# Graph attention on one core: another order of exps, unit ends and gathers, and other engines for the one-hots

## The chip, the cores and the metric

The kernel runs on one core of a Trainium2 chip. A core has a matrix engine (PE, TensorE), a vector engine (DVE), a scalar engine (ACT), GpSimd (POOL) and a sync engine (SP), which works as a queue of DMA starts here. Each engine takes its instructions in order and waits on semaphores of the others. The metric is the device time of one execution in microseconds; the time given is the median of ten.

## What is computed

The reference applies four graph layers in a row to 6250 nodes with 128 features and 100000 edges, sorted by destination. Each stands behind a layer norm and a relu and is added to x:

```python
h = relu(layernorm(x)); x = x + L0(h)   # mean over neighbours, two weights, relu
h = relu(layernorm(x)); x = x + L1(h)   # filter of distances, product over neighbours
h = relu(layernorm(x)); x = x + L2(h)   # three mean layers
h = relu(layernorm(x)); x = x + L3(h)   # three attention layers
```

The change touches the attention, and what is prepared for it during L2. One attention layer, over all edges and one loop per node:

```python
h = x @ W
alpha = leaky_relu((h @ a_src)[s] + (h @ a_dst)[d] + ea_full @ We @ a_edge, 0.2)
ex = exp(alpha - segment_max(alpha, d)[d])
coef = ex / (segment_sum(ex, d)[d] + 1e-16)
out = segment_sum(h[s] * coef[:, None], d) + bias
```

Behind each come a leaky relu and a batch norm over the nodes.

## The kernel before

**Tables.** A node is row p (0 to 124) and column l (0 to 49, `T` = 50) of a table in SBUF. Attention takes its destinations in two parts. The first 3200 nodes (64 rows) are "early": they are summed by matmuls with one-hots. The rest are "late": their edges are gathered one by one.

**Early nodes.** They make five groups (`GP`) of 128 windows. A window holds five nodes (`NW`) and up to 128 edge slots, among them the five loops. For one window PE multiplies two one-hots that have the slots on their 128 partitions. The edge one-hot (128 x 125) says in which row a slot's source lies, weighted by the slot's coefficient; the node one-hot (128 x 250) says to which of five nodes the slot belongs and in which of 50 columns its source lies. The product `cnt` (125 x 250) holds the weights with which table rows go into the window's nodes. `split_edges` (line 2270) walks through 160 steps a layer, 32 a group, each of four windows:

- `ready` (L2420), two steps ahead: it makes node one-hots `hot_n` and edge one-hots `hot_c` and `hot_l`, three buffers of each. Even windows of a step are kept in f32. Odd windows are in the rounded form fp32r and have the coefficient in two parts, `coef_h` and `coef_l`. DVE makes `hot_n` of the even windows by comparing slot numbers with `id_t` (L116); ACT converts those of the odd windows from fp8 tiles that were loaded (L2435), and makes the edge one-hots with the coefficient as scale (L2436); DVE makes `hot_l` of both odd windows at once (L112).
- PE: six `cnt` matmuls of the program (eight rows in the trace, L2623 and L2624). `cnt` has two buffers in PSUM.
- `merged` (L2604): one step later ACT copies `cnt` into `m` (L2607).
- `product` (L2442): eight steps are a unit (32 windows). During the next unit PE multiplies the table by `m` in 50 matmuls (L2447), seven a step. Behind the last, the unit's end: bias on ACT (L2450), leaky relu and batch statistics on DVE (L121, L2452), and a copy into `y_t` on ACT (L2454), all three emitted in step 1 of a unit, ahead of that step's `merged`.
- In the first 20 steps of a group, `source_terms` (L2340) fetches the sources' terms for the next group with small matmuls and reductions on DVE; in the last 12, `softmax` (L2365) makes its coefficients, a piece a step.

**Late nodes.** POOL gathers their edges' table rows with indirect DMAs, 392 a layer, 128 edges each (`fetch`, L2458). `late` (L2477) takes them in blocks of eight: `weights` (DVE: terms, running maximum, exponents), an exp on ACT (L2502), rows times exp on DVE (L112), and eight dependent accumulations on DVE (`acc`, L121), then the store to `late_hist`. It is a generator that advances by 196 pieces in 150 steps, four a block: the exp; rows times exp; four accumulations; four more with the store and `weights` of the block after. Three buffers of rows; `fetch_to` (L2470) releases gathers by the same count, and each is tied to PE's last instruction emitted before it (`clocked`). After the last block comes a serial tail: `late_fix`, then gathers of the sums and the late nodes' ends.

**Ahead of attention.** During L2 a generator `early_edges` (L2030) makes the one-hots in fp8 and stores them in DRAM. `woven` (L1575) interleaves it with PE's units of L2, some nine pieces a unit. Each of 80 iterations handles eight windows: eight `ee_hot` (L2028), one `ee_col` (L2149), four `ee_node` of the odd windows (L2028) and one `ee_hot_t`. A unit of L2 ends with a DVE product `agg` (L112), on which PE's `nt` (L1564) waits a little later.

**What sets the order.** `chain` (L1611) ties the instructions of PE, DVE and ACT in the order in which the program emits them, so an instruction that waits holds up all behind it on its engine. SP's and POOL's follow their queues.

The functions that the diff touches:

Of the kernel before, what the change touches and what calls it, by code (L numbers as in the profile page):

```python
# [22 lines left out]
P = 125  # L23
# [28 lines left out]
def kernel(ctx: ExitStack, tc: tile.TileContext, a: dict, out: bass.AP):  # L52
# [1778 lines left out]
    node_dram = [dram.tile([128, 64 * T * NW], F8, name=f"node{g}") for g in range(GP)]  # L1831
# [10 lines left out]
    class Late:  # L1842
# [3 lines left out]
        def __init__(self, pool):  # L1846
# [12 lines left out]
            self.id_t = pool.tile([128, GP, 128], F32, name="l_id_t")  # L1859
# [170 lines left out]
    def early_edges(lt):  # L2030

        with tc.tile_pool(name="ee", bufs=1) as pool, tc.tile_pool(name="ee_ps", bufs=1, space=PSUM) as ps:
# [59 lines left out]
            for g in range(GP):  # L2092
# [177 lines left out]
    def split_edges(lt, i, first, wp, pool, ps, mv, sc):  # L2270
# [94 lines left out]
        def softmax(g, al_s, of, al, wide):  # L2365

            if not of:
# [41 lines left out]
        def nodes_ready(step):  # L2409

            g, w0 = step // 32, step % 32 * 4
            if w0 % WB == 0:
                lt.hot = pool.tile([128, WB, 128], F8, name="hot")
                nc.sync.dma_start(lt.hot.rearrange("p w h -> p (w h)"), hot_dram[g][:, w0 * 128:(w0 + WB) * 128])
            half_n = pool.tile([128, 2, T * NW], F8, name="half_n")
            nc.sync.dma_start(half_n.rearrange("p w n -> p (w n)"),
                              node_dram[g][:, w0 // 2 * T * NW:(w0 + 4) // 2 * T * NW])
            return half_n

        def ready(step, half_n=None):  # L2420
# [21 lines left out]
        def product(unit, m):  # L2442
# [3 lines left out]
            for l in range(T):  # L2446
                nc.tensor.matmul(o, lhsT=hst[:, l, :D], rhs=m[:P, l, :], start=(l == 0), stop=(l == T - 1))  # L2447
                yield
            z = pool.tile([128, NW, 32], F32, name="z_w")
            nc.scalar.activation(z, o, AF.Identity, bias=bias, scale=1.0)  # L2450
# [3 lines left out]
            nc.scalar.activation(y_t[:, t0:t0 + NW, w0 % P1:w0 % P1 + 32], z, AF.Copy)  # L2454

# [14 lines left out]
        def fetch_to(pieces):  # L2470

            nonlocal fetched
            while fetched < min(C2, 2 * pieces + 16, NB * ((done - 1) // 4 + 3)):
                next(fetches)
                fetched += 1

        def late():  # L2477
# [20 lines left out]
            ahead = weights(0)  # L2498
            for c0 in range(0, C2, NB):
                rows, ex, now = ahead  # L2500
                yield
                nc.scalar.activation(ex, ex, AF.Exp)  # L2502
# [108 lines left out]
        for step in range(steps):  # L2611
# [21 lines left out]
            counted = cnt  # L2633
            if step + 2 < steps:
                hots.append(ready(step + 2))
# [10 lines left out]
            while done < min(4 * (C2 // NB) + 1, (step + 1) * pace):  # L2646
                next(edges_late)
                done += 1
            if done >= 4 * (C2 // NB) + 1:
# [3 lines left out]
        for _ in before:  # L2653
            pass
        before = product(steps // 8 - 1, m)
# [11 lines left out]
        for _ in before:  # L2667
            pass
        held = ps.tile([128, 3, D], F32, name="held", tag="x_ps", bufs=2)
# [475 lines left out]
```

## Time and profile before

| | us |
|---|---|
| median of 10 executions | 4815.62 (4808.55 to 4823.71) |
| the profiled execution | 4825.44 |
| its span, first to last instruction | 4823.0 |
| PE, DVE, ACT, POOL busy | 4160.7, 4043.6, 3306.5, 2851.1 |
| attention layers, about | 2811 to 3471, 3471 to 4135, 4135 to 4795 |

| group of instructions, by form | count | mean ns | idle before it, us, and what ended most of it |
|---|---|---|---|
| L116 DVE `hot_n`, 128x250 | 960 | 363 | 5.3 |
| L112 DVE `hot_l`, 128x250 | 480 | 416 | 1.0 |
| L2435 ACT `hot_n`, 128x250 | 960 | 402 | 27.5, DMA of `half_n` |
| L2436 ACT `hot_c`, 128x125 | 1920 | 391 | 0.1 |
| L2607 ACT `m`, 125x1000 | 480 | 989 | 14.9 |
| L1653 ACT `as_f`, 128x1000 from fp8 | 390 | 1028 | 273.1, DMA of `piece` |
| L2624 PE `cnt` | 2880 | 359 | 122.4, ACT `m` 118.4 |
| L2454 ACT `y_t` | 60 | 339 | 86.6, DVE `z_w` |
| L2502 ACT `ex` | 147 | 213 | 212.4, DVE `ex` 211.8 |
| L2028 DVE `ee_node`, 128x250 | 320 | 363 | 0.4 |
| L67 POOL gathers of `rows`, attention | 1176 | 1015 | 537.2, issue 277.0 |

How to read it: busy time counts an engine as busy while an instruction runs, so neighbours that overlap count once; the mean is that of one instruction, begin to end. On a full engine the next may begin before the last one's recorded end, so start to start can be less than the mean. "Idle before" is the engine's own idle time just ahead of such instructions; what ended it is inferred from semaphores, and "issue" means that the profile shows nothing that was waited for. The view by windows gives per stretch the busy time of each engine with its instructions in brackets, PE's granted clock, the mean busy share of the 16 DMA engines, and GB/s. Lines of the view of waits read: who waits for whom, us in total, times, longest. Lines of the timeline: start, length, engine, line.

### The profile page before, as it was taken

The page shows a single profiled execution, that of the slowest core. Times are in us where ns is not written, and L with a number is a line of the kernel's source. Part 1 is how long each engine was busy: PE and PEld are TensorE (multiplying, and loading weights), DVE is VectorE, ACT ScalarE, POOL GpSimd, SP SyncE. Part 2 cuts the span into 40 slices and gives each one's busy share as a digit, 9 for nine tenths or more (in the row PEclk, how much of TensorE's full clock was granted, in tenths as well). Part 3 has the DMA queues.
Part 4 walks back from the last instruction along what each step waited for, and adds up shares of the span by engine and source line. Part 5 has one row for each costly group of instructions (what it writes and reads, how often), then busy time and mean ns, then how long its engine had stood idle before and what let it go on. Part 6 is the DMA issues. An engine that isn't in the chain of part 4 may idle for free. (4 is left out here: it accounts for less than half of the span.)

```text
span 4823.0 us, 84662 instructions
## 1 busy us (share of the span) xinstructions
PE 4160.7 (86%) x25786; PEld 2987.4 (62%) x25786; DVE 4043.6 (84%) x12029; ACT 3306.5 (69%) x6467; POOL 2851.1 (59%) x2848
## 2 busy tenths in 40 slices
PE   1499998888888869899999979999889999799996
PEld 0255544444444435555555569889779899698896
DVE  7999869999999964677868869899699997798985
ACT  5466658888888857543345567778577778687784
POOL 1365007777777754656737537777367676477772
PEclk9999996666666659999999999999999999899998
DMA  4344336555666647899989955555455554455554
GB/s 99 102 153 157 99 109 221 203 195 204 202 207 201 187 126 223 259 292 277 295 251 295 281 169 162 154 157 155 139 146 156 158 157 136 146 161 153 154 151 111
DMA packets 577362, 868.53 MB, mean 180 GB/s; under 512 B 206555, under 2 KB 451739, under 8 KB 568450
## 3 DMA queue, kind: packets, MB, share of 16 engines
q1 hardware_dynamic: 483459, 674.15, 44.0%
q0 software_dynamic: 91104, 186.95, 15.0%
q8 instruction: 205, 3.36, 0.3%
q10 hardware_dynamic: 2332, 1.93, 0.2%
q14 instruction: 262, 2.15, 0.1%
HBM read 563.92 MB, written 298.68 MB: 179 GB/s over the span
## 5 line engine op out<-in xcount | busy, mean ns | idle before, releaser
L67 POOL DMA_INDIRECT rows<-gtable,l_src x1176 | 1193.1, 1015 | 537.2 <-issue 277.0
L67 POOL DMA_INDIRECT rows<-table,f_src x784 | 781.2, 996 | 282.4 <-issue 231.5
L2447 PE MATMUL o<-m,hst 125*128 125x160 f32 x6000 | 916.7, 304 | 0.0
L67 POOL DMA_INDIRECT s_rows<-table,s_src x660 | 659.5, 999 | 346.4 <-issue 164.2
L2624 PE MATMUL cnt<-hot_n,hot_c 128*125 128x250 f32 x2880 | 755.3, 359 | 122.4 <-ACT m L2607 118.4
L2447 PEld LDWEIGHTS o<-m,hst 125*128 125x128 f32 x6000 | 855.4, 194 | 0.0
L1653 ACT ACTIVATE as_f<-piece 128x1000 fp32r<-128x1000 fp8e4 x390 | 380.7, 1028 | 273.1 <-DMA piece<-adj 183.9
L2624 PEld LDWEIGHTS cnt<-hot_n,hot_c 128*125 128x125 f32 x2880 | 450.2, 192 | 160.4 <-ACT m L2607 130.4
L2607 ACT ACTIVATE m<-cnt 125x1000 f32<-125x1000 f32 x480 | 474.7, 989 | 14.9 <-PE cnt L2624 13.4
L923 PE MATMUL z<-w,s 128*128 128x128 f32 x1568 | 347.3, 391 | 153.2 <-DVE s L121 148.6
L2623 PE MATMUL cnt<-hot_n,hot_l 128*125 128x250 f32 x960 | 453.3, 472 | 0.0
L121 DVE SCALAR_TENSOR_TENSOR acc<-acc,ex,rows 128x130 f32<-128x130 f32 x1173 | 414.5, 353 | 33.8
L923 PEld LDWEIGHTS z<-w,s 128*128 128x128 f32 x1568 | 294.5, 281 | 232.9 <-DVE s L121 232.3
L1544 PE MATMUL o<-as_f,of_two 128*128 128x500 f32 x1560 | 415.1, 412 | 13.1 <-ACT as_f L1653 11.9
L1407 ACT ACTIVATE adj<-cnt 128x1000 fp8e4<-128x1000 f32 x250 | 305.5, 1222 | 176.0 <-PE cnt L1406 170.3
L2435 ACT ACTIVATE hot_n<-half_n 128x250 fp32r<-128x250 fp8e4 x960 | 386.4, 402 | 27.5 <-DMA half_n<-node 27.1
L2436 ACT ACTIVATE hot_c<-hot,coef_t 128x125 f32<-128x125 fp8e4 x960 | 375.6, 391 | 0.1
L2436 ACT ACTIVATE hot_c<-hot,coef_h 128x125 fp32r<-128x125 fp8e4 x960 | 374.9, 391 | 0.0
L902 PE MATMUL z<-bf,w 128*128 128x512 f32 x392 | 354.3, 1002 | 8.9 <-ACT bf L868 8.9
L1544 PE MATMUL o<-adj,parts 128*128 128x500 fp8e4 x1500 | 358.6, 377 | 0.1
L1544 PEld LDWEIGHTS o<-as_f,of_two 128*128 128x128 f32 x1560 | 295.4, 192 | 85.0 <-ACT as_f L1653 16.5
L868 ACT ACTIVATE soft<-z 128x512 f32<-128x512 f32 x392 | 222.0, 586 | 164.2 <-PE z L923 163.7
(628 smaller groups left out, 8114.2 us busy)
## 6 DMA issues: line engine op xcount, KB each, us to landing
piece<-adj SPq DMA_DIRECT2D x360, 250.0 KB
late_hist<-acc SPq DMA_DIRECT2D x147, 455.0 KB
dist<-ew_dram SPq DMA_DIRECT2D x48, 1024.0 KB
sum_hist<-s_acc SPq DMA_DIRECT2D x132, 320.0 KB
adj<-adj SPq DMA_DIRECT2D x10, 3125.0 KB
hot<-hot SPq DMA_DIRECT2D x240, 128.0 KB
half_n<-node SPq DMA_DIRECT2D x480, 62.5 KB
ea<-in_edge_attr SPq DMA_DIRECT2D x54, 512.0 KB
```

What stands on the lines that cost most here:

```text
L67: return nc.gpsimd.indirect_dma_start(out=dst, out_offset=None, in_=table, in_offset=bass.IndirectOffsetOnAxis(ap=idx, axis=0))
L121: nc.vector.scalar_tensor_tensor(o, x, s, y, op0=op0, op1=op1)
L902: nc.tensor.matmul(z1, lhsT=w1, rhs=st["bf"][:, i % 2 * HB:(i % 2 + 1) * HB, :], start=False, stop=True)
L923: nc.tensor.matmul(z2[:, j, :], lhsT=s1[:, j, :], rhs=w2, start=False, stop=j == HB - 1)
L1544: yield nc.tensor.matmul(o[:, :n], lhsT=parts.columns(l, 1, s)[:, 0, :], rhs=adj(l), start=(l == 0 and s == 0), stop=(l == T - 1 and s == ...
L1653: nc.scalar.activation(made[-1], piece[:, at:at + n], AF.Copy)
L2435: nc.scalar.activation(hot_n[k][:, h, :], half_n[:, h, :], AF.Copy)
L2436: nc.scalar.activation(hot_c[k][:, h, :], hot[:, w, :], AF.Copy, scale=(high if k else coef)[:, w0 + w:w0 + w + 1])
L2447: nc.tensor.matmul(o, lhsT=hst[:, l, :D], rhs=m[:P, l, :], start=(l == 0), stop=(l == T - 1))
L2607: nc.scalar.activation(m[:P, :, :, u * 4:u * 4 + 4].rearrange("p l k q -> p k l q"), cnt[:P, :, :T * NW].rearrange("p w (k l) -> p k l w", ...
L2623: nc.tensor.matmul(o, lhsT=hot_l[:, h, :], rhs=hot_n[k][:, h, :], start=True, stop=False)
L2624: nc.tensor.matmul(o, lhsT=hot_c[k][:, h, :], rhs=hot_n[k][:, h, :], start=k == 0, stop=True)
```

## The change

- Node one-hots are now made ahead for all windows. In `early_edges` DVE compares four windows at once (128x1000, both operands spread), twice in each of the 80 iterations, in place of four comparisons; the table in DRAM and its stores double. `id_t` (f32, kept) becomes `id_b` (bf16, in the pool of that stage).
- In `ready`, ACT converts the node one-hots of two windows at a time (500 columns), even and odd ones alike; the tile `half_n` holds four windows. DVE weights the edge one-hots in pairs, by a product with the spread coefficients.
- A unit's end becomes a generator in three parts, run in steps 1, 2 and 4 of a unit, behind `merged`.
- `late`: `weights` of the next block stands before the accumulations, its exp among them, so that the pieces of a block are: rows times exp; `weights`; four accumulations; exp and four more with the store. The last piece of a block is one later than before. The store is one DMA in place of two.
- `fetch_to`: up to 20 gathers ahead in place of 16, with the rule of buffers shifted by one piece; that rule now binds.
- `softmax`: one more pause among its five exps, from the second group on.

```diff
@@ early_edges
-                for x, x_t in ((hi, hi_t), (lo, lo_t), (place, lt.id_t[:, g, :])):
+                id_b = pool.tile([128, 128], BF16, name="ee_id_b")
+                for x, x_t in ((hi, hi_t), (lo, lo_t), (place, id_b)):
...
-                    node = pool.tile([128, WB // 2, T * NW], F8, name="ee_node", bufs=2)
-                    for w in range(0, WB, 2):
-                        n = w0 + w + 1
-                        one_hot(node[:, w // 2, :], slot_b, lt.id_t[:, g, n:n + 1])
-                    nc.sync.dma_start(node_dram[g][:, w0 // 2 * T * NW:(w0 + WB) // 2 * T * NW],
-                                      node.rearrange("p w n -> p (w n)"))
+                    for n0 in range(w0, w0 + WB, 4):
+                        node = pool.tile([128, 4, T * NW], F8, name="ee_node", bufs=2)
+                        nc.vector.tensor_tensor(node, slot_b[:, None, :].to_broadcast([128, 4, T * NW]),
+                                                id_b[:, n0:n0 + 4, None].to_broadcast([128, 4, T * NW]), OP.is_equal, saturate=False)
+                        nc.sync.dma_start(node_dram[g][:, n0 * T * NW:(n0 + 4) * T * NW], node.rearrange("p w n -> p (w n)"))
@@ softmax
                                      accum_out=node[:, 1, k:k + 1])
+                if parted and k == NW // 2:
+                    yield
@@ nodes_ready
-            half_n = pool.tile([128, 2, T * NW], F8, name="half_n")
+            half_n = pool.tile([128, 4, T * NW], F8, name="half_n")
@@ ready
-            for w in range(4):
-                k, h = w % 2, w // 2
-                if k == 0:
-                    ts(hot_n[k][:, h, :], lt.slot[:, :T * NW], lt.id_t[:, g, w0 + w:w0 + w + 1], OP.is_equal)
-                else:
-                    nc.scalar.activation(hot_n[k][:, h, :], half_n[:, h, :], AF.Copy)
-                nc.scalar.activation(hot_c[k][:, h, :], hot[:, w, :], AF.Copy,
-                                     scale=(high if k else coef)[:, w0 + w:w0 + w + 1])
+            by = hot.rearrange("p (h k) c -> p k h c", k=2)
+            for k, of in enumerate((coef, high)):
+                nc.scalar.activation(hot_n[k], half_n.rearrange("p (h k) n -> p k h n", k=2)[:, k], AF.Copy)
+                tt(hot_c[k], by[:, k], of[:, w0:w0 + 4].rearrange("p (h k) -> p k h", k=2)[:, k, :, None].to_broadcast([128, 2, P]), OP.mult)
@@ product, its end
+            ends.append(unit_end(unit, g, w0, o))
+        def unit_end(unit, g, w0, o):
             z = pool.tile([128, NW, 32], F32, name="z_w")
             nc.scalar.activation(z, o, AF.Identity, bias=bias, scale=1.0)
+            yield
             stt(z, z, 0.01, z, OP.mult, OP.max)
             nc.vector.bn_stats(stats[:, unit, :], z.rearrange("f k q -> f (k q)"))
+            yield
             t0 = w0 // P1 * GP * NW + g * NW
             nc.scalar.activation(y_t[:, t0:t0 + NW, w0 % P1:w0 % P1 + 32], z, AF.Copy)
@@ fetch_to
-            while fetched < min(C2, 2 * pieces + 16, NB * ((done - 1) // 4 + 3)):
+            while fetched < min(C2, 2 * pieces + 20, NB * ((done - 2) // 4 + 3)):
@@ late
             ahead = weights(0)
+            yield
+            nc.scalar.activation(ahead[1], ahead[1], AF.Exp)
+            yield
             for c0 in range(0, C2, NB):
                 rows, ex, now = ahead
+                more = c0 + NB < C2
+                tt(rows, rows, ex[:, 0, :, None].to_broadcast([PL, NB, W]), OP.mult)
                 yield
-                nc.scalar.activation(ex, ex, AF.Exp)
+                if more:
+                    ahead = weights(c0 + NB)
                 yield
                 acc = pool.tile([PL, NB, W], F32, name="acc")
-                tt(rows, rows, ex[:, 0, :, None].to_broadcast([PL, NB, W]), OP.mult)
-                yield
                 for j in range(NB):
+                    if j == NB // 2:
+                        yield
+                        if more:
+                            nc.scalar.activation(ahead[1], ahead[1], AF.Exp)
...
-                    if j == NB // 2 - 1:
-                        yield
                 nc.vector.tensor_copy(acc[:, :, AL], now)
-                bulk(bass.AP(tensor=late_hist.tensor, offset=late_hist.offset + c0 * W, ap=[[C2 * W, PL], [1, NB * W]]),
-                     acc.rearrange("p c f -> p (c f)"))
-                if c0 + NB < C2:
-                    ahead = weights(c0 + NB)
-            yield
+                nc.sync.dma_start(bass.AP(tensor=late_hist.tensor, offset=late_hist.offset + c0 * W, ap=[[C2 * W, PL], [1, NB * W]]),
+                                  acc.rearrange("p c f -> p (c f)"))
+                yield
@@ the steps
                 merged(step - 1, m, counted)
             counted = cnt
+            if u in (1, 2, 4):
+                end_some()
```

`end_some` runs one part of the oldest unit's end; behind the loop all that are left are run.

More of the change, by code (lines that the diff above doesn't have):

```diff
@@ L1830 @@
     of_dram = [dram.tile([128, NW * WCAP], BF16, name=f"of{g}") for g in range(GP)]
-    node_dram = [dram.tile([128, 64 * T * NW], F8, name=f"node{g}") for g in range(GP)]
+    node_dram = [dram.tile([128, 128 * T * NW], F8, name=f"node{g}") for g in range(GP)]
     ale_dram = [[dram.tile([128, WCAP], F32, name=f"ale{i}_{g}") for g in range(GP)] for i in range(3)]
@@ L1858, in __init__ @@
             self.slot = pool.tile([128, C2], F32, name="l_slot")
-            self.id_t = pool.tile([128, GP, 128], F32, name="l_id_t")
             self.vecs = [pool.tile([128, 6], F32, name=f"l_vecs{i}") for i in range(3)]
@@ L2365, in softmax @@
         def softmax(g, al_s, of, al, wide):
+            parted = not of
             if not of:
@@ L2414, in nodes_ready @@
                 nc.sync.dma_start(lt.hot.rearrange("p w h -> p (w h)"), hot_dram[g][:, w0 * 128:(w0 + WB) * 128])
-            half_n = pool.tile([128, 2, T * NW], F8, name="half_n")
-            nc.sync.dma_start(half_n.rearrange("p w n -> p (w n)"),
-                              node_dram[g][:, w0 // 2 * T * NW:(w0 + 4) // 2 * T * NW])
+            half_n = pool.tile([128, 4, T * NW], F8, name="half_n")
+            nc.sync.dma_start(half_n.rearrange("p w n -> p (w n)"), node_dram[g][:, w0 * T * NW:(w0 + 4) * T * NW])
             return half_n
@@ L2448, in product, with end_some @@
                 yield
+            ends.append(unit_end(unit, g, w0, o))
+        ends = []
+        def unit_end(unit, g, w0, o):
             z = pool.tile([128, NW, 32], F32, name="z_w")
             nc.scalar.activation(z, o, AF.Identity, bias=bias, scale=1.0)
+            yield
             stt(z, z, 0.01, z, OP.mult, OP.max)
             nc.vector.bn_stats(stats[:, unit, :], z.rearrange("f k q -> f (k q)"))
+            yield
             t0 = w0 // P1 * GP * NW + g * NW
             nc.scalar.activation(y_t[:, t0:t0 + NW, w0 % P1:w0 % P1 + 32], z, AF.Copy)
+        def end_some():
+            if ends:
+                if next(ends[0], 0) == 0:
+                    ends.pop(0)
         NB, given, order = 8, [], Pace(0)
@@ L2645, in split_edges @@
             fetch_to((step + 1) * pace)
-            while done < min(4 * (C2 // NB) + 1, (step + 1) * pace):
+            while done < min(4 * (C2 // NB) + 2, (step + 1) * pace):
                 next(edges_late)
                 done += 1
-            if done >= 4 * (C2 // NB) + 1:
+            if done >= 4 * (C2 // NB) + 2:
                 for _ in islice(edges_late, 2):
@@ L2654, in split_edges @@
             pass
+        while ends:
+            end_some()
         before = product(steps // 8 - 1, m)
@@ L2668, in split_edges @@
             pass
+        while ends:
+            end_some()
         held = ps.tile([128, 3, D], F32, name="held", tag="x_ps", bufs=2)
```

## The prediction

> **What bounds the kernel now.** I read the page first (span 4823.0 us; PE 86%, DVE 84%, ACT 69% busy), then busy time by windows, because the two stages that the change touches have different limits. First the loop of the first attention layer, one window for each of its five groups of 32 steps:
>
> ```profile
> core 0: us, PE busy (x) PEld busy (x) DVE busy (x) ACT busy (x) POOL busy (x), PEclk, DMA share, GB/s
> 2856.00:2975.00 119.00, 101.73 (x939) 95.42 (x940) 109.64 (x330) 95.37 (x266) 89.45 (x88) 0.94 0.57 157
> 2975.00:3095.00 120.00, 111.65 (x1045) 105.77 (x1044) 105.85 (x319) 89.99 (x249) 85.51 (x85) 0.99 0.56 155
> 3095.00:3214.00 119.00, 110.68 (x1042) 105.34 (x1041) 107.39 (x325) 93.39 (x260) 87.26 (x83) 0.97 0.56 156
> 3214.00:3330.00 116.00, 110.33 (x1044) 105.53 (x1043) 107.76 (x324) 91.51 (x253) 85.01 (x84) 0.99 0.59 161
> 3330.00:3434.00 104.00, 98.18 (x647) 93.97 (x646) 74.44 (x243) 86.29 (x233) 59.96 (x61) 0.97 0.46 127
> ```
>
> PE and DVE are equally full in four groups of five; only in the last, which prepares no next group, DVE is light. The two other layers look alike. Next who waited for whom in the first four groups, 2856 to 3330 us:
>
> ```profile
> ACT ex L2502 <- DVE ex L121: 65.7, 32, 4.2
> ...
> PE cnt L2624 <- ACT m L2607: 36.3, 18, 5.1
> ACT y_t L2454 <- DVE z_w L121: 23.7, 14, 4.0
> ...
> DVE coef_l L112 <- ACT coef_t L2405: 6.2, 4, 2.4
> DVE z_w L121 <- ACT z_w L2450: 5.6, 5, 3.1
> DVE al L112 <- issue: 5.4, 24, 0.6
> ```
>
> So PE stalls on `merged` (ACT m), because ACT, which works in order, stands before it at an exp or a unit's end that waits for DVE. The engine waited for in the end is DVE. DVE itself hardly waits: 430.6 us busy of 474, and of the 43.4 idle this view names 22.8; the rest are gaps between dependent instructions too short to be listed.
>
> Second, the layers before (1860 to 2811 us), where the one-hots are made beside PE's matmuls; three windows, each from one `agg` of a unit to the next:
>
> ```profile
> 2480.50:2508.80 28.30, 28.30 (x130) 17.97 (x129) 12.12 (x45) 16.47 (x19) 5.23 (x4) 1.00 0.79 222
> ...
> 2543.30:2573.40 30.10, 29.73 (x133) 18.22 (x132) 28.39 (x97) 16.86 (x19) 23.08 (x24) 1.00 0.99 313
> ...
> 2668.80:2700.90 32.10, 30.21 (x130) 18.78 (x129) 30.08 (x103) 17.16 (x21) 21.78 (x22) 0.95 0.98 292
> ```
>
> PE sets the pace, but in the busy units DVE is 94% full and the DMA engines 98%, while in others DVE is half empty.
>
> **Part 1, the edge and node one-hots in the loop.** A step loses two DVE instructions (node one-hots, L116) and four on ACT (edge one-hots, L2436), and gains two products on DVE; the two ACT copies of 250 become two of 500. The new products have the form of today's `hot_l` (128x250, fp8 times a spread f32). What counts on a full engine is start to start:
>
> ```profile
> 2999.26 1.23 DVE L112 TENSOR_TENSOR rows<-rows,ex 128x1040 f32<-128x1040 f32 x1
> ...
> 3000.41 0.60 DVE L116 TENSOR_SCALAR hot_n<-l_slot,l_id_t 128x250 f32<-128x250 f32 x2
> ...
> 3000.93 0.41 DVE L112 TENSOR_TENSOR hot_l<-hot,coef_l 128x250 fp32r<-128x250 fp8e4 x1
> ...
> 3001.26 0.57 DVE L112 TENSOR_TENSOR one<-x_ps,col 128x400 f32<-128x400 f32 x1
> ```
>
> Two one-hots take 3000.93-3000.41 = 0.52 us, one product 3001.26-3000.93 = 0.33. Two products less two one-hots: +0.14 us a step, 4.5 a group, 17.9 over four groups. ACT is relieved: 2x402+4x391 = 2368 ns a step before; a copy of 500 lies between the rows of 250 (402) and 1000 (1028 ns, L1653), about 610, so 1220 after. ACT is not the limit, so this saves only what its lateness costs. The node tiles read double: at a DMA share of 0.57 I cost it at nothing; ACT waited for them 27.1 us in all, and with ACT early that wait has cover. If not, 28 waits of 1 us are the price.
>
> The Trainium skill, "VectorE: DVE Perf Modes", perf-mode tier table, lets `tensor_scalar` run at twice the rate of `tensor_tensor` in fp32, which speaks against this swap. This trace does not agree: 250 elements in 0.26 us is one a cycle of its 0.96 GHz. By the page a one-hot would take about (58+125)/0.96 = 0.19 us (estimate) and the swap would cost 0.14 us a step more, 18 us a layer; I go by the rows.
>
> **Part 2, the order of exp, `weights` and unit ends.** The order of the built kernel puts `weights` a step ahead of its exp, and a unit's end on ACT, DVE, ACT in three different steps. ACT's 65.7 and 23.7 us of waiting go; so do DVE's waits for ACT: 6.2 + 5.6 + 0.9 (`rows` for ex) = 12.7 us. What is late next is DVE. Four groups: 430.6 + 17.9 busy, 43.4 - 12.7 = 30.7 idle that stays, 479.2 against 474: **+5.2 us a layer**. Bounds: -13 (the swap hidden) to +18 (no wait goes).
>
> **Part 3, gathers and last group.** `fetch_to` now releases the eight gathers of a block together, when the block three before is done, and `weights` wants them a piece earlier: six pieces, 4.6 steps, some 17 us, after release. They take 8x(0.95+0.30) = 10 us on POOL, 2.3 to 3.0 to land (chain of waits), and wait for PE's last matmul of their step, up to 3.7. That is 13 to 17 of 17, so DVE will wait now and then: I take **+3 a layer** (0 to +40, a wait of 1 us at each of 40 blocks). In the last group gathers bind already (8.1 us of waits of `al` there). The last block's `weights` now stands ahead of the previous block's eight accumulations, which came first before: 8 x 0.38 (row of `acc`: 414.5+33.8 us by 1173) = **+3 a layer** into the serial tail (0 to +3). PE's stall on `merged` in the last group, 4.8 us in the first layer, goes, but only some lies on the path: **-2** (-5 to 0). The late table's store as one DMA saves an issue of SP, off the path; the extra pause in softmax ends two steps before its coefficients are wanted: nothing.
>
> Sum in attention: 3 x (5.2+3+3-2) = **+28 us**.
>
> **Part 4, node one-hots for all, in the layers before.** 80 times, four one-hots of 250 become two operations of 1000:
>
> ```profile
> 2363.74 0.56 DVE L2149 TENSOR_TENSOR ee_col<-ee_slot_b,ee_lo_t 128x400 fp8e4<-128x400 bf16 x1
> 2364.23 1.91 DVE L121 SCALAR_TENSOR_TENSOR s_acc<-s_acc,s_same,s_rows 128x128 f32<-128x128 f32 x5
> 2366.06 1.20 DVE L2028 TENSOR_SCALAR ee_node<-ee_slot_b,l_id_t 128x250 fp8e4<-128x250 bf16 x4
> 2367.18 0.96 DVE L2028 TENSOR_SCALAR ee_hot_t<-ee_rows,ee_here 128x1024 fp8e4<-128x1024 uint8 x1
> ```
>
> `ee_col` has the new form: 400 elements in 0.49 us. `rows` above does 1040 in 1.15, so an element costs 0.66/640 = 1.04 ns and 1000 cost 1.11. Two: 2.22 against 1.12 to 1.16 for the four: +1.08 us, x80 = **86 us of DVE** from 2060 to 2760. I added it to each of the 22 windows between `agg`s (0 to 5 iterations in each). The sum exceeds the window in ten, by 18 us together (30.10: 28.39+5.40 = 33.8; 32.10: 35.5); if DVE can fill only 95%, as in its fullest window, by 36 in twelve. PE then waits at `nt<-agg`, where it already waits 20.9 us in the run. The other windows swallow the rest. The doubled stores add 80 x 128 KB = 10.2 MB; in windows at a share of 0.96 to 1.00 and some 310 GB/s each iteration's 0.128 MB costs 0.4 us, some 16 us in nine windows, mostly the same ones that DVE lengthens, so not added. I take **+30** (0 to 86).
>
> **Sum.** 28 + 30 = +58. The profiled execution took 4825.4 us (span 4823.0), 0.2% over the median 4815.6 of the ten runs; it would take 4883, and the median **4874 us**. Own range with the bounds of the parts mixed: 4830 to 4915.
>
> **Rivals.** (a) *The order wins.* PE's idle time for `merged` is 118.4 us in the page. If DVE's idle time is mostly slack and not gaps, ACT's freedom returns half of it and the lulls before hide part 4: 4815.6 - 59 = **4757**. It decides once DVE's work with its gaps stays under PE's 111 us a group; against it stands the fourth group, 116 us with DVE busy 107.8 before 4.5 are added. (b) *Hidden on both sides*: -4 and 0, **4812**. Against it: the 94% windows. (c) *Part 4 at full price*, since waits of DVE for ACT and SP's in-order queue (`piece` loads stand behind the node stores, which wait for DVE) spoil the lulls: 28 + 86, **4930**. (d) *Late gathers* at every block of four groups, 1 us each: 4874 + 3 x 37 = **4985**; for it, the 13 to 17 of 17 us; against it, a stalled DVE falls back towards PE, which shortens the wait for PE.
>
> **Chances.** Forecast 0.48, (a) 0.13, (b) 0.13, (c) 0.19, (d) 0.07. About 0.2%, 10 us, can be told from no change: faster 0.13, same 0.13, slower 0.74. The range leaves out (d) and most of (a): 4800 to 4935.
>
> **What would show it.** Right: DVE at 94% or more in the first four groups, 114, 110, 112 and 112 us busy; ACT under 60% there with no waits of `y_t` for `z_w`; groups of 117 to 121 us; `ee_node` 2.2 us a pair, units at 2543 and 2668 longer by 3 to 5 us with PE waiting for `agg`. Wrong: groups of 112 us with PE at 98% (a); units unchanged (b); `al` waiting for `rows` over 10 us a layer (d). A product of fp8 by f32 faster than 0.33 us would also undo it.

## The result and the profile after

The changed kernel takes **4942.97 us** (median of 8 runs, 4936.09 to 4955.84) against 4817.29 for the kernel before in the same comparison (28 runs): ratio **1.0265**, 95% interval 1.0255 to 1.0275. It is slower, as forecast, by twice the forecast: 126 us for 58. The profiled execution has a span of 4945.1 us (before 4823.0, +122.1).

Three marks in the trace divide these 122 us (1.2 us more lie outside the rows): the first `ee_node`, the first `hot_l` of a layer, and the first matmul into `held` behind its loop and tail.

| stretch | before | after | difference |
|---|---|---|---|
| start to first `ee_node` | 2059.7 | 2054.9 | -4.8 |
| first `ee_node` to first `hot_l` (the layers before) | 797.0 | 858.1 | **+61.1** |
| first `hot_l` to `held`, three layers | 614.6, 611.1, 612.1 | 631.6, 632.6, 638.2 | **+64.6** |

So both halves are larger than forecast: 61 for 30, and 65 for 28. A stretch is read from one profiled execution. How far to trust it shows in runs on such chips that leave a stretch's code as it was: the layers before took 797.0, 790.9 and 793.5 us, attention 1837.8, 1841.4 and 1837.7, and the start, which no edit touches, 2038 to 2060.

**The layers before.** The view by windows over the second stretch, first of the kernel before, then of the changed one (columns: window, length, then busy time and instructions of PE, PEld, DVE, ACT and POOL, PE's granted clock, DMA share, GB/s):

```profile
2059.70:2856.70 797.00, 759.50 (x3802) 463.24 (x3801) 604.36 (x2017) 379.46 (x507) 424.83 (x428) 0.98 0.87 271
```

```profile
2054.90:2913.00 858.10, 777.56 (x3801) 471.79 (x3799) 688.18 (x1856) 379.85 (x506) 489.61 (x427) 0.95 0.86 264
```

PE does the same 3801 matmuls. Its idle time grows from 37.5 to 80.5 us (+43.0), and the matmuls themselves take 18.1 us longer, at a mean clock of 0.95 in place of 0.98: 43.0 + 18.1 = 61.1, all of it. The waits name who is late, first in the kernel before (2055 to 2765 us), then in the changed one (2055 to 2820 us):

```profile
PEld nt L1564 <- DVE agg L112: 16.0, 11, 4.4
...
PE nt L1564 <- DVE agg L112: 8.3, 5, 3.6
```

```profile
PEld nt L1564 <- DVE agg L112: 62.8, 16, 6.9
...
PE nt L1564 <- DVE agg L112: 50.1, 15, 6.1
```

PE's matmuls wait for the end of a unit on DVE 15 times in place of 5, for 41.8 us more: nearly all of the 43.0. Why a wait also makes the matmuls slower shows in three short windows around one of these pauses (5.4 us, ended at 2409.8 by `agg`); columns: window, length, PE busy with its matmuls in brackets, clock, DMA share, GB/s.

```profile
2404.00:2410.00 6.00, 0.58 (x2) 0.71 0.86 253
2410.00:2414.00 4.00, 4.00 (x10) 0.58 0.80 239
2414.00:2418.00 4.00, 4.00 (x22) 1.00 0.94 306
```

For some 4 us behind the pause PE is granted 0.58 of its clock and gets through ten matmuls, and then through 22 in as long. By the trace's clock record, which holds only the full and the half clock here, the half clock is granted for 37.5 us in 7 stretches of this part before, and for 88.7 us in 17 after. PE is busy for 29.9 and 68.4 us of that; half of the 38.5 us more is 19.2, about the 18.1 by which the matmuls got longer.

**Attention.** The five groups of the first layer in the changed kernel:

```profile
2913.00:3031.00 118.00, 101.57 (x940) 94.30 (x940) 105.22 (x311) 68.79 (x126) 85.89 (x84) 0.96 0.59 170
3031.00:3151.00 120.00, 110.66 (x1032) 103.98 (x1031) 109.83 (x326) 69.70 (x127) 83.25 (x84) 0.97 0.58 169
3151.00:3270.00 119.00, 110.13 (x1026) 103.90 (x1026) 108.19 (x318) 70.71 (x127) 86.21 (x82) 0.97 0.59 172
3270.00:3391.00 121.00, 111.72 (x1037) 105.16 (x1036) 109.13 (x326) 69.71 (x127) 85.49 (x84) 0.97 0.58 170
3391.00:3500.00 109.00, 100.17 (x649) 92.75 (x648) 76.35 (x246) 65.52 (x112) 63.48 (x62) 0.98 0.49 145
```

ACT is at 58%, as meant. But DVE is not full: 432.4 us busy of 478 in the first four groups (90%), and even in the last group, where DVE is 70% busy, the loop got longer. The waits of the first four groups (longer ones of ACT and POOL left out at the top):

```profile
...
ACT hot_n L2433 <- DMA half_n<-node: 67.8, 37, 5.7
POOL rows L67 <- PE x_ps L2356: 33.3, 17, 6.0
...
ACT ex L2525 <- DVE ex L121: 25.1, 13, 6.1
DVE al L112 <- DMA rows<-gtable,l_src: 24.5, 17, 3.8
PE x_ps L2356 <- DMA hot_t<-hot_t: 20.3, 12, 5.8
```

and in the kernel before, in its first four groups (2857 to 3326 us):

```profile
POOL rows L67 <- PE x_ps L2357: 10.6, 13, 1.6
...
DVE al L112 <- DMA rows<-gtable,l_src: 2.3, 12, 0.2
...
PE x_ps L2357 <- DMA hot_t<-hot_t: 2.0, 4, 0.8
```

ACT's waits for DVE went for the most part, as forecast (`ex` 65.7 to 25.1, `y_t` is gone), and PE's wait for `m` with them (36.3 to 6.2). In their place DVE waits for gathered rows, 24.5 us here and 17.0 in the last group, against 2.3 and 8.1 before; and PE waits for loads of `hot_t`. These share SP's queue with loads of `hot`, which wait for a buffer that DVE still reads (SP waits 91.6 us for `hot_l` there); that this is what delays them is not shown.

Some of the runs below were on chips on which the kernel before itself takes 5344 to 5413 us, with waits of PE named issue that the runs shown so far don't have. They are kept apart, under 4, and no difference in time is taken across.

### The profile page after: what moved, and what is told of

Read it like the earlier page. It is cut to its first block, busy times and chain, and to the rows that moved or that the text cites. A ratio compares the mean times of both kernels' runs of the same rounds, so it can differ in the third digit from the quotient of the medians.

```text
span 4945.1 us, 81847 instructions
## 1 busy us (share of the span) xinstructions
PE 4204.7 (85%) x25786; PEld 3000.2 (61%) x25786; DVE 4156.0 (84%) x11869; ACT 2978.4 (60%) x4547; POOL 2933.8 (59%) x2848
## 5 line engine op out<-in xcount | busy, mean ns | idle before, releaser
L67 POOL DMA_INDIRECT rows<-gtable,l_src x1176 | 1209.0, 1028 | 575.9 <-issue 307.4
L67 POOL DMA_INDIRECT s_rows<-table,s_src x660 | 719.7, 1090 | 335.1 <-issue 163.9
L2433 ACT ACTIVATE hot_n<-half_n 128x500 f32<-128x500 fp8e4 x960 | 539.2, 612 | 301.3 <-DMA half_n<-node 300.3
L118 DVE TENSOR_SCALAR run<-acc,f_same,f_fresh 128x128 f32<-128x128 f32 (+1 forms) x783 | 313.2, 400 | 14.4
L1544 PE MATMUL o<-piece,of_three 128*128 128x500 fp8e4 x1200 | 290.0, 385 | 2.2 <-ACT of_three L1121 1.7
```

Source lines behind the costliest of these rows:

```text
L67: return nc.gpsimd.indirect_dma_start(out=dst, out_offset=None, in_=table, in_offset=bass.IndirectOffsetOnAxis(ap=idx, axis=0))
L118: nc.vector.tensor_scalar(o, x, s1, s2, op0=op0, op1=op1)
L1544: yield nc.tensor.matmul(o[:, :n], lhsT=parts.columns(l, 1, s)[:, 0, :], rhs=adj(l), start=(l == 0 and s == 0), stop=(l == T - 1 and s == ...
L2433: nc.scalar.activation(hot_n[k], half_n.rearrange("p (h k) n -> p k h n", k=2)[:, k], AF.Copy)
```

## The experiments

The question is which part costs what. The theory after the traces: part 4 costs the layers before 61 us through DVE, and attention is set by late gathers. Rivals: DVE's extra products are the whole loss in attention; the doubled stores are that of part 4.

**1. The one-hots alone (parts 1 and 4), and the order alone (parts 2 and 3).** The changed kernel is cut in two: `early_edges`, `nodes_ready` and `ready` are those of after in the one, and of before in the other; all else goes the other way.

> The one-hot parts alone (1 and 4) once more, since in the first call the kernel before took 5411 us, 12% more than in its shown runs, with waits of TensorE named issue that those runs do not have. Expected where the kernel before takes 4816 us: theory (part 4 costs the layers before 55 us, the new order most of the rest): first hot_n load 55 us later, attention +10 to +25 us in all, about 4890 us. Rival (VectorE's extra products are the loss in attention): attention +55 to +70, about 4935 us.

> The new order alone (parts 2 and 3), once more for the same reason. Theory (late gathers are the price in attention): the layers before as before, waits of al for rows 25 to 45 us a layer, attention +20 to +40 us, about 4845 us. Rival (VectorE's extra products): attention 0 to -20, about 4805 us. Rival (a) of the prediction: 4757 us.

| | time (ratio, its interval) | before there | first `ee_node` to `hot_l` | three layers | DVE waits ahead of `al`, by layer |
|---|---|---|---|---|---|
| one-hots alone | 4914.11 (1.0213, 1.0194 to 1.0233) | 4815.02 | 862.7 (+65.7) | 1861.6 (+23.8) | 19.7, 18.0, 20.9 |
| order alone | 4823.52 (1.0022, 1.0011 to 1.0033) | 4815.02 | 790.9 (-6.1) | 1857.2 (+19.4) | 42.5, 46.2, 41.9 |
| both: the change | 4942.97 | 4817.29 | 858.1 (+61.1) | 1902.4 (+64.6) | 41.6, 44.6, 44.5 |
| (before) | | | 797.0 | 1837.8 | 16.9, 15.3, 12.7 |

Part 4 alone accounts for the layers before. In attention each half costs some 20 us, and both together 21 more than their sum. DVE's waits for rows come with the order: some 131 us in three layers with it, 45 before, and 59 with the one-hots alone. The rival (products are all) falls: it wanted 55 to 70 in the first row and a gain in the second. The one-hots alone took 4914 in place of the 4890 expected: part 4 took 66 and not 55, and the median lies 8 us above the profiled run. The order alone took 4824 in place of 4845: its waits for rows came as the theory said, and cost the least that it had allowed.

**2. Rows in time.** A fourth buffer for gathered rows, and the release a block earlier, in the changed kernel and in the order alone (which, so that it fits, also has one buffer in place of two for the products on the way to `al_s`):

```diff
-                    given.append(pool.tile([128, NB, W], F32, name="rows", bufs=3))
+                    given.append(pool.tile([128, NB, W], F32, name="rows", bufs=4))
-            while fetched < min(C2, 2 * pieces + 20, NB * ((done - 2) // 4 + 3)):
+            while fetched < min(C2, 2 * pieces + 28, NB * ((done - 2) // 4 + 4)):
```

> The changed kernel with four buffers of gathered rows in place of three, and gathers released a block earlier (ten pieces ahead of the weights, not six). Theory (late gathers cost attention what the order alone lost, 19 us, and the 21 us that order and one-hots lost together beyond their sum): waits of al for rows fall from 42 to 20 us a layer or less, attention 40 us shorter than in the changed kernel, about 4903 us. Rival (VectorE is full, and fills the time it no longer waits with its delayed work; or the loads behind it in SP's queue set the pace): within 10 us of 4943 us.

> The new order with the old one-hots, with four buffers of gathered rows and the earlier release (and one buffer in place of two for the products on the way to al_s, so that it fits). Theory (late gathers are what the order lost): waits of al 15 us a layer as before the change, attention 20 us shorter than with the order alone, and shorter than before the change by what ScalarE's freedom is worth, 0 to 30 us in all: about 4800 us. Rival (the gathers' waits only fill time in which VectorE would wait for others): 4815 to 4830 us.

The changed kernel with rows in time takes **4851.26** (before 4815.43; ratio 1.0080, interval 1.0063 to 1.0097), 92 us less than without, more than twice what was expected. Attention takes 599.0, 600.2 and 601.4 us a layer: 101.8 less than the change, and 37.2 less than before it. The first four groups:

```profile
2910.00:3365.00 455.00, 425.95 (x4047) 402.43 (x4046) 430.79 (x1276) 277.79 (x503) 349.57 (x338) 0.99 0.62 180
```

```profile
ACT hot_n L2433 <- DMA half_n<-node: 60.7, 36, 6.2
...
PE x_ps L2356 <- DMA hot_t<-hot_t: 6.3, 10, 1.2
...
DVE al L112 <- DMA rows<-gtable,l_src: 3.1, 3, 2.3
```

Now DVE is 95% busy (430.8 of 455): here is the full DVE that the prediction had taken for granted. PE's waits for `hot_t` shrank from 20.3 to 6.3 without any edit to those loads, so most of them followed from the late rows. (SP's waits for `hot_l` fell less, from 91.6 to 75.9.) ACT's waits for `half_n` are nearly as long as in the changed kernel and seem to cost nothing: ACT has 177 of 455 us to spare. And PE's clock is back at 0.99.

The order alone with rows in time takes **4733.22** (ratio **0.9840**, interval 0.9819 to 0.9861), 82 us faster than the kernel before: a version that beats both. Attention takes 1754.4 us, 83.4 less than before. Its first four groups:

```profile
2832.00:3275.00 443.00, 423.35 (x4044) 401.20 (x4042) 417.70 (x1277) 364.60 (x1011) 339.00 (x338) 0.99 0.59 166
```

PE is 96% busy, so little is left there to win. The three terms of attention can be read off now: order with rows in time -83.4, one-hots on top +46.2 (1800.6 - 1754.4), late rows on top +101.8; their sum is +64.6. The first includes whatever the buffer would be worth without the order.

The two pairs also show what a wait of DVE for rows costs here. In the changed kernel its waits ahead of `al` fell from 130.7 to 33.0 us in the three layers, by 97.7, and attention by 101.8. In the order alone they fell from 130.6 to 26.4, by 104.2, and attention by 102.7. So the price was the length of the waits, nearly one for one.

**3. What part 4 pays with.** The kernel before with one half of part 4's cost each: four more one-hots an iteration to a spare tile, or every node store issued twice.

```diff
+                    spare = pool.tile([128, WB // 2, T * NW], F8, name="ee_spare", bufs=2)
+                    for w in range(0, WB, 2):
+                        one_hot(spare[:, w // 2, :], slot_b, lt.id_t[:, g, w0 + w:w0 + w + 1])
```

```diff
+                    nc.sync.dma_start(spare_dram[g][:, w0 // 2 * T * NW:(w0 + WB) // 2 * T * NW],
+                                      node.rearrange("p w n -> p (w n)"))
```

> The kernel before with four more one-hots of 250 in each of the 80 iterations of the layers before, written to a spare tile that nothing reads: VectorE's added time of part 4 (1.12 us an iteration against 1.08), without its doubled stores. Theory (VectorE's time is the price of part 4): first hot_n load 45 to 60 us later, attention unchanged, about 4868 us. Rival (the doubled stores, which keep the next node tile and the loads behind them waiting, are half of it or more): 25 us or less, about 4835 us.

> The kernel before with each store of node one-hots issued a second time, to a table that nothing reads: the doubled stores of part 4 without VectorE's added time. Theory (VectorE's time is the price of part 4): 0 to 10 us, about 4820 us. Rival (the stores): 25 to 50 us, about 4850 us.

DVE's time alone: 4879.43 (ratio 1.0130, interval 1.0112 to 1.0148); the stretch takes 858.7, +61.7. That is the whole of part 4's price. The stores alone: 4856.58 (1.0091, interval 1.0074 to 1.0109); the stretch takes 836.0, +39.0, where 0 to 10 were expected. So each alone costs much, and both together no more than DVE's alone. A likely reason is that a PE that waits for DVE gives the transfers the time that they need: in the changed kernel ACT waits less for its adjacency pieces than before, 99.9 us for 167.5. It was not tested by itself. With the stores alone these waits are the ones that grow most. Of PE's idle time there, 27.3 us more than before, 10.9 are waits for what ACT makes of the pieces, 5.5 for pieces themselves and 9.4 for `agg` (ACT's waits of the kernel before from 2055 to 2765 us, then with doubled stores from 2044 to 2800 us):

```profile
ACT as_f L1653 <- DMA piece<-adj: 167.5, 54, 12.5
```

```profile
ACT as_f L1653 <- DMA piece<-adj: 264.6, 77, 12.2
```

**4. Runs on the other chips** (before at 5344 to 5413 us). They cover the two halves of the change and the changed kernel with rows in time (the same kernels as above), the unit's end alone, the buffer alone, the buffer with the unit's end, the old order with gathers released as in the change, and the faster version with another release. The edits that are new:

```diff
@@ old order, gathers of a block released together, six pieces ahead
-            while fetched < min(C2, 2 * pieces + 16, NB * ((done - 1) // 4 + 3)):
+            while fetched < min(C2, 2 * pieces + 24, NB * ((done - 3) // 4 + 3)):
@@ old order, four buffers
+            while fetched < min(C2, 2 * pieces + 24, NB * ((done - 1) // 4 + 4)):
@@ new order, four buffers, two gathers a piece
+            while fetched < min(C2, 2 * pieces + 22, NB * ((done - 2) // 4 + 4)):
```

The two halves of the change, and the changed kernel with rows in time:

> The one-hot parts alone (parts 1 and 4: all node one-hots made and stored in the layers before, converted on ScalarE; edge one-hots weighted in pairs on VectorE), with the old order of exp, weights, unit ends and gathers. Theory (two separate prices: the layers before lose 55 us to part 4; in attention the changed kernel loses most of its 65 us to the gathers, which the new order releases later): first hot_n load 55 us later than before, attention only +10 to +25 us in all three layers, VectorE waiting for rows no more than before (15 us a layer), about 4890 us. Rival (VectorE's extra products are the whole loss in attention): attention +55 to +70 here too, about 4935 us.

> The new order alone (parts 2 and 3: unit ends in three steps, softmax pause, weights a step ahead of its exp, gathers released in whole blocks), with the one-hots made as before. Theory (late gathers are the price in attention): the layers before as before; VectorE waits for rows 25 to 45 us a layer as in the changed kernel, attention +20 to +40 us, about 4845 us. Rival (VectorE's extra products): attention 0 to -20, about 4805 us. Rival (a) of the prediction, the order wins half of PE's waits: about 4757 us.

> The changed kernel with four buffers of gathered rows in place of three, and gathers released a block earlier to match. Theory (late gathers are the price in attention): waits of al for rows fall from 42 us a layer to 17 or less, attention gains 30 to 50 us in all, about 4905 us. Rival (VectorE's extra products, or the loads behind them in SP's queue): rows arrive in time but PE waits as long, within 10 us of 4943 us.

The unit's end alone:

> Only the unit's end in three steps and the pause in the softmax; late edges, gathers and one-hots as before. Theory (ScalarE's waits for z_w, 24 us in the first four groups of a layer, hold up the merge of the counts, on which PE waits 36 us there): PE's waits on m fall by a third, 5 to 10 us a layer gained, about 4795 us. Rival (VectorE sets the end, PE's waits are slack): within 0.2% of before, 4806 to 4825 us.

The buffer alone, and with the unit's end:

> The kernel before with the fourth buffer of gathered rows and the earlier release alone (nine pieces ahead of the weights), old order, old one-hots. Theory (the old order had its rows 5 to 13 us early, so the buffer is worth little without the new order; the gain of the order with the buffer, 82 us, is the order's): waits of al fall by 5 us a layer, 0 to 15 us gained, about 4808 us. Rival (the buffer is the gain, in any order): attention 60 to 85 us shorter, about 4740 us.

> The kernel before with the fourth buffer of gathered rows and the earlier release alone, once more, since in the call before this one the kernel before took 5402 us. Theory (the old order had its rows 5 to 13 us early, so the gain of the order with the buffer is the order's): 0 to 15 us gained, about 4808 us. Rival (the buffer is the gain, in any order): attention 60 to 85 us shorter, about 4740 us.

> The kernel before with the fourth buffer of gathered rows and the earlier release alone. Where the kernel before takes 4816 us: theory (the old order had its rows 5 to 13 us early, so the gain of the order with the buffer is the order's): 0 to 15 us gained, about 4808 us. Rival (the buffer is the gain, in any order): attention 60 to 85 us shorter, about 4740 us. Where it takes 5410 us: again 30 us slower, as in the two runs there.

> The same with the unit's end in three steps and the pause in the softmax, late edges in the old order. Theory (of PE's 36 us of waits on m in the first four groups of a layer, the exps that wait for weights on VectorE cause more than the unit ends do, by their waits of 66 to 24 us): a quarter of the order's gain, 15 to 30 us, about 4790 us. Rival (the unit ends on ScalarE are the larger part): 50 us or more, 4765 us or less.

> The same with the unit's end in three steps and the pause in the softmax, late edges in the old order, once more for the same reason. Theory: a quarter of the order's gain, 15 to 30 us, about 4790 us. Rival (the unit ends on ScalarE are the larger part): 50 us or more, 4765 us or less.

The release in eights in the old order:

> The kernel before, old order and old one-hots, with its gathers released as in the change: the eight of a block together, six pieces ahead of its weights. Theory (the late release costs by itself): waits of al of 30 us a layer or more, attention 20 to 60 us longer, about 4850 us. Rival (the release costs only together with the new order, in which ScalarE no longer waits for VectorE): within 10 us of before, about 4816 us.

> The kernel before, old order and old one-hots, with its gathers released as in the change: the eight of a block together, six pieces ahead of its weights. Where the kernel before takes 4816 us: theory (the late release costs by itself): waits of al of 30 us a layer or more, attention 20 to 60 us longer, about 4850 us. Rival (it costs only together with the new order): within 10 us of before, about 4816 us. Where it takes 5410 us: again 5% slower, as in the run there.

The faster version, two gathers a piece:

> The new order with the old one-hots and four buffers of gathered rows, its gathers released two a piece, the last of a block seven pieces ahead of the weights, and no longer eight at once. Where the kernel before takes 4816 us: theory (what counts is that rows arrive in time): as fast as with whole blocks, 4725 to 4745 us; rival (the early first gathers are needed): 4760 us or more. Where it takes 5410 us: theory (there the burst of eight gathers is what costs 5%): 5350 to 5440 us; rival (it is the order): 5650 us or more.

| kernel, and how it releases gathers | ratio to before there |
|---|---|
| one-hots alone, two a piece | 1.0023 |
| unit's end alone, two a piece | 0.9994 |
| buffer alone, two a piece, three runs | 1.0061, 1.0067, 1.0078 |
| buffer and unit's end, two a piece, two runs | 1.0065, 1.0098 |
| new order with buffer, two a piece | 0.9986 |
| old order, eight at once, six pieces ahead, two runs | 1.0509, 1.0535 |
| new order alone, eight at once | 1.0520 |
| changed kernel with rows in time, eight at once | 1.0564 |

None of these ratios can stand for the chips of the result: there the one-hots alone cost 1.0213 (here 1.0023) and the order alone 1.0022 (here 1.0520). What was forecast for these chips came about: the buffer alone 29 us slower for 30, the release in eights 5.1% for 5, and two a piece 5342 us, just under the 5350 to 5440 of the theory and far from the 5650 of its rival. The unit's end brought nothing that can be told from none here, alone (0.9994) or beside the buffer (1.0065 and 1.0098). The rows part into two classes, by one property: whether eight gathers are released at once. The new order with four buffers is at 0.9986 with two a piece, and in the old order the release in eights alone costs 5%, so there it is not the order. But DVE's waits for rows are not what it pays with: the changed kernel with rows in time waits 0.8, 2.4 and 1.0 us ahead of `al` in its three layers, and still loses 5.6%. PE stops on its own issue instead; its waits in the first four groups of the old order, first with the buffer, then with the release in eights:

```profile
PE o L2447 <- issue: 24.6, 36, 1.1
PE x_ps L2357 <- issue: 23.9, 33, 2.0
```

```profile
PE o L2447 <- issue: 50.2, 75, 1.2
PE x_ps L2357 <- issue: 48.3, 64, 1.9
```

Why a burst of gathers should hold up PE's issue on these chips, and why they are slower at all, the profile does not show. It stays open. The version that wins 1.6% on the chips of the result releases in eights and was not run on these. Two things stay open for the chips of the result: the release in eights in the old order, and the buffer without the new order. For the second there is an estimate: before, DVE waited 16.9, 15.3 and 12.7 us a layer ahead of `al`, and if a wait is worth its length, as in the two pairs under 2, the buffer could have saved at most 45 of the 82 us.

## Why the prediction was wrong, step by step

**Right in direction, and too small by half.** In attention two terms were far off, in opposite directions, so that it is luck that its +28 came as near to the measured 65 as it did:

| us a layer | forecast | measured |
|---|---|---|
| the swap of one-hots (part 1) | +17.9 | +15.4 |
| order and unit ends (part 2) | -12.7 | -27.8, with the buffer |
| late gathers (part 3) | +3 | +33.9 |
| last group | +1 | not apart from the others |
| sum | +9.2 | +21.5 |

Its steps:

- *A product for a one-hot costs 0.33 for 0.26 us* (part 1): right. `hot_c` measured 0.33 start to start. But that 0.26 us for 250 elements is "one a cycle", and so speaks against the page's doubled rate, is very likely a misreading. The trace of before has such comparisons in three sizes, with median durations of 278 ns for 128 elements (`ee_hot`), 342 for 250 (`ee_node`) and 746 for 1024 (`ee_hot_t`): 0.52 ns an element, half of the 1.04 that the prediction found for products, and a fixed part that weighs much in small ones. The sum went by the rows and does not depend on this. The swap was put at 17.9 us a layer of DVE; with the old order DVE is busy 438.9 us in four groups on average for 425.6, +13.3. As a price in time it was 7.9 a layer under the old order and 15.4 under the new one with rows in time.
- *ACT's waits go, and 12.7 us of DVE's* (part 2): right in the main. `z_w`, `coef_l` and `rows` for `ex` no longer wait; `ex` on ACT still does, for 25.1 us. The step from there failed: "What is late next is DVE", with 30.7 us idle that stays. 45.6 stayed, since something else was late next.
- *Gathers, "I take +3 a layer (0 to +40 ...)"* (part 3): **this is the step that failed.** Its working had found no slack to speak of, 13 to 17 us of 17, with PE in the chain, and then took a price near nothing. The measured price is 101.8 us, 34 a layer, near the upper end and near what rival (d) worked out (37), though not as a wait of 1 us at every block: in the first layer 24 waits, of up to 4.7 us. That rival got 7 in 100 on the argument that "a stalled DVE falls back towards PE, which shortens the wait for PE". The waits speak for the reverse: DVE works in order, so a wait of `al` delays the one-hots behind it, PE waits, and the next gathers are tied to PE. POOL's waits for PE's `x_ps` rose from 10.6 to 33.3 us in the first layer's four groups, and with rows in time they are 2.0. That this loop is why the rows stayed late was not tested apart. In the last group, gathers followed each other without a break in both kernels, 74 and 75 us for the last seven blocks of the first layer, so what they were late by was never made up.
- *"-2" for PE's stall on `merged` in the last group, "+3" for the accumulations*: they drown. The loop's last groups grew by 5 to 14 us, with 17 to 18 us of waits ahead of `al`.
- *Part 4, "I take +30"*: **the other step that failed**, by 31 us. DVE's bill was right (1.11 us start to start for 1.11; DVE +83.8 us for 86), and the rule that only windows without spare time pay held in the main: the twelve windows that DVE overfills at 95% grew by 51 us, the other ten by 8. By 95% filling it said 36 us of waits at `nt`; 41.8 came. I took less than that, and the term that was missing altogether is the clock: 18.1 us. The units at 2543 and 2668 grew by 5.3 and 6.9 us for "3 to 5".
- *The doubled stores, "some 16 us ... not added"*: that they don't add to DVE's was right; alone they cost 39.
- *The node tiles read double, at nothing*: nothing speaks against it. ACT waited 67.8 us for them in four groups, and hardly less, 60.7, where the time was won back.
- *Rival (a), the order wins 59 us*: in attention its mechanism fits, and the gain is larger than it said, 83 us, but only with rows in time and with what the fourth buffer is worth by itself; PE's wait for `m` fell from 36.3 to 5.7 us in four groups there. That the lulls hide part 4 is wrong. The likeliest case and (a) and (d) were held to exclude each other; the gain of (a) and the price of (d) are both there, and in the order alone they nearly cancel.

The Trainium skill, "TensorE: Matmul & The Clock Gate", Part 1, says that the array's clock is halved after an idle window of about 3.4 us and restored after as long a busy one. The trace agrees on the two levels and on the length of the slow stretch, some 4 us above. It differs on the trigger: of twelve pauses of 2.0 to 3.5 us between 1860 us and attention, all shorter than 3.4, nine were followed by a half clock. The prediction's own rows show clocks of 0.94 and 0.95, and it counted pauses only by their own length.

## What to carry to other kernels

When a wait is removed by doing something earlier, work out the slack of what that something consumes, as a time and with its bounds; if the slack is near nothing, reckon with a price near the far end, as here, where the consumer paid for its waits in full (102 us for 98) and its lateness may have delayed the next input too (rows, DVE, PE, release of rows). A change that frees one engine and starves another can look like a loss of the wrong part: separate the parts before undoing them, here a buffer and an earlier release turned +2.65% into +0.8%, and without the one-hots into -1.6%. A pause of PE can cost more than its length: in the layers before, 43 us of added pauses cost 61.

## What the runs showed of the hardware

- Most pauses of PE of 2 us or more were followed by a stretch at half clock (nine of twelve between 2.0 and 3.5 us), in multiples of 3.41 us in the clock record; in the layers before, 43.0 us more of pauses brought 18.1 us more of matmul time.
- Comparisons with a value per partition, written as fp8, took 0.52 ns an element on DVE (342 ns for 250, 746 for 1024), products of two tensors 1.04, each with a fixed part; so at 250 elements, 0.26 against 0.33 us start to start, the doubled rate is hardly seen.
- Half the bill of a loaded stage can be free, whichever half: DVE's added 90 us (80 x 1.12) alone cost 62, the added stores (80 x 128 KB) alone 39, both together 61.
- On some chips the same kernel takes 5344 to 5413 us in place of 4815, with PE stopping on its own issue, and there eight gathers released at once cost 5 to 6% whatever the order (1.0509 to 1.0564); with two a piece the same changes stay within 1% (0.9986 to 1.0098). On the chips of the result the order with eight at once is at 1.0022, or 0.9840 with rows in time.
